# Layer 0 of a four-layer graph network: visiting order of the row tiles, ring of adjacency buffers, first load in pieces

## The chip, the cores and the metric

The kernel runs on one core of one Trainium2 chip. The metric is device time in microseconds (us), the median of several executions of the whole program, which is one launch. The program computes four layers of a graph network; the change touches the first of them.

## The reference, cut to what matters

There are N = 2708 nodes with D = 128 features (x), and a dense 2708 x 2708 float32 matrix adj of which under one per cent is non-zero. Layer 0 is

```python
h = jnp.maximum(_layernorm(x, axis=-1), 0.0)
x = x + _L0_gnn_ref(h, adj)

def _L0_gnn_ref(X, H):
    msg = jnp.matmul(H.T, X)
    inv_deg = 1.0 / H.sum(axis=0)
    inv_deg = jnp.where(jnp.isinf(inv_deg), 0.0, inv_deg)
    return msg * inv_deg[:, None]
```

Layer 1 sums gelu messages over the edges (weights from adj), layer 2 is a GRU cell on adj @ h, and layer 3 is an attention masked by adj > 0. All four read adj: layers 2 and 3 need it transposed, and layer 1 works from lists of its non-zero entries. Layer 0 prepares both forms while it computes its own result.

## The kernel before, in words

adj is cut into 22 row tiles of 128 rows (`NT`); the last, tile 21, has 20 rows. They are visited in `GROUPS`: five sets of four tiles and a last short set of two (20 and 21). For each row tile n layer 0 does five things:

- `load_row_tile(n)` (L254, issued by SyncE, SP) loads 128 x 2708 floats, 1354 KB.
- `aggregate_rows(n, ci)` (L297, TensorE) accumulates msg for six column chunks of at most 512, with the normalised rows `h` as the stationary operand. The six accumulators stay in PSUM for the whole layer.
- `list_row_tile(n)`: for each of 22 column blocks of 124 columns VectorE finds the eight largest values (MAX8, L283) and their positions (FIND_INDEX8, L285). The blocks near the diagonal are read from a copy, `near`, that GpSimd (POOL) makes without the diagonal (L265, L266); POOL also puts the diagonal itself in `dg` (L270). Both tiles have two buffers. The two last row tiles have only their near blocks scanned here; the rest is scanned in layer 1.
- `sign_sums(n)` (L290, L292, ScalarE): counts of non-zero entries, and the diagonal summed from `dg`.
- `turn_blocks(gi, j)`, for each of 22 column tiles j of a set: TensorE transposes one 128 x 128 block of each row tile of the set into a PSUM tile `p_T` (L309; there are two such banks), ScalarE copies it to `aT` and sums it for the degrees (L313), and SP stores it to `adjT` in DRAM (L314). `aT` has eight buffers.

The order on every engine is written out by hand, in `tc.manual_schedule()`. One set after the other is visited. In the first visit all accumulations stand ahead of the transposes; in the others they are interleaved with the 22 steps j. In a visit of four tiles each of steps 1, 6, 11 and 16 issues the scan of one tile, steps 3, 8, 13 and 18 its sign sum, and from the second visit on steps 3, 7, 11 and 15 the load of a tile of the next set. At step 20 `normal_rows` makes the next set's `h` (L137, `hs` in the profile). The first two tiles' scans and sign sums and the sums over x (`sum_rows`, `sum_squares`) stand in the first visit ahead of its transposes.

The row tiles lie in two buffers of a set each (4 x 2708 floats per partition), so the first load of a set waits until all four tiles of the set two visits before are done with. Eight row tiles are loaded at the start, with the rest of x after the second.

The layer ends with the counts of the first four tiles (L350, L352), six copies of the accumulators to `hT`, three by VectorE and three by ScalarE (L355), and the degrees from the sums (L360 to L364), which need the last `aT`. Layer 1 then begins with transposes of `hT` (L767).

The statistics of x for the first four tiles (L118 to L131, with a power on POOL, L121) are issued before, outside the hand-written order; where they stand among the first scans is decided by the scheduler.

Of the kernel before, what the change touches and what calls it, by code (L numbers as in the profile page):

```python
# [20 lines left out]
F32 = mybir.dt.float32  # L21
BF16 = mybir.dt.bfloat16
AF = mybir.ActivationFunctionType
# [7 lines left out]
P = 128  # L31
N = 2708
D = 128
NT = (N + P - 1) // P
# [9 lines left out]
JB = 124  # L44
# [3 lines left out]
GROUPS = [(t, min(4, NT - t)) for t in range(0, NT, 4)]  # L48
# [3 lines left out]
def size(t):  # L52
    return min(P, N - t * P)


def width(b):
    return min(JB, N - b * JB)
# [3 lines left out]
def listed_layers(ctx: ExitStack, tc: tile.TileContext, x, adj, w, out, flag):  # L61
    nc = tc.nc
# [23 lines left out]
    ident = const.tile([P, P], F32, name="ident")  # L86
# [60 lines left out]
    def span(t, k):  # L147

        return t * P, min(k * P, N - t * P)
# [17 lines left out]
    total = keep.tile([P, NT], F32, name="total")  # L167
# [24 lines left out]
    for q in range(2):  # L192
        nc.gpsimd.tensor_copy(xb[q][:, :, 4 * S : 4 * S + R], part.unsqueeze(1).to_broadcast([P, NB, R]))

    LATER = NT - 2
    AT_ONCE = 3
    late_blocks = []
# [7 lines left out]
    with tc.tile_pool(name="l0c", bufs=1) as fix:  # L205
# [29 lines left out]
        def normal_rows(g):  # L235
            t, k = GROUPS[g]
            scale_rows(tiles_of(h, t, k), tiles_of(xs, t, k), rstd[:, t - 4 :], shifts[:, t - 4 :], AF.Relu)

        with (
            tc.tile_pool(name="l0", bufs=2) as rows,  # L240
            tc.tile_pool(name="l0k", bufs=2) as pool,
            tc.tile_pool(name="l0t", bufs=8) as turned,
            tc.tile_pool(name="l0p", bufs=1, space=PSUM) as acc,
        ):
            accs = [acc.tile([P, CH], F32, name=f"acc{c}") for c in range(len(CHUNKS))]
            sets, marks = {}, {}

            def load_row_tile(n):
                gi, q, m = n // 4, n % 4, size(n)
                if q == 0:  # L250
                    sets[gi] = rows.tile([P, 4, N], F32, name="a")
                if m < P:
                    nc.gpsimd.memset(sets[gi][:, q, :], 0.0)
                nc.sync.dma_start(sets[gi][0:m, q, :], adj[n * P : n * P + m, :])  # L254

            def list_row_tile(n):

                m = size(n)
                a = sets[n // 4][:, n % 4, :]
# [10 lines left out]
                nc.gpsimd.tensor_tensor(marks[n][:, 0:m], a[:, d0 : d0 + m], ident[:, 0:m], ALU.mult)  # L270

                def block(b):
                    if b0 <= b <= b1:
                        return near[:, b * JB - c0 : b * JB - c0 + width(b)]
                    return a[:, b * JB : b * JB + width(b)]

                blocks = [b for b in range(NB) if not b0 <= b <= b1] + list(range(b0, b1 + 1))
                if n >= LATER:
                    late_blocks.extend((n, b) for b in range(NB) if not b0 <= b <= b1)
                    blocks = range(b0, b1 + 1)  # L280
                for k in range(0, NB, 2):
                    for b in blocks[k : k + 2]:
                        nc.vector.max(val[:, n, b, :], block(b))  # L283
                    for b in blocks[k : k + 2]:
                        nc.vector.max_index(col[:, n, b, :], val[:, n, b, :], block(b))  # L285

            def sign_sums(n):
                m = size(n)
                sign = pool.tile([P, N], BF16, name="sign")
                nc.scalar.activation(sign, sets[n // 4][:, n % 4, :], AF.Sign, accum_out=total[:, n : n + 1])  # L290
                dg = marks.pop(n)[:, 0:m]
                nc.scalar.activation(dg, dg, AF.Copy, accum_out=own[:, n : n + 1])  # L292

            def aggregate_rows(n, ci):
                c, cw = CHUNKS[ci]
                m = size(n)
                nc.tensor.matmul(  # L297
                    accs[ci][:, 0:cw], h[0:m, n, :], sets[n // 4][0:m, n % 4, c : c + cw],
                    start=(n == 0), stop=(n == NT - 1),
                )  # L300

            def turn_blocks(gi, j):
                g0, gk = GROUPS[gi]
                i0, iw = span(g0, gk)
                k = size(j)
                p = bank("p_T")
                for q in range(gk):
                    m = size(g0 + q)
                    nc.tensor.transpose(  # L309
                        p[0:k, q * P : q * P + m], sets[gi][0:m, q, j * P : j * P + k], ident[0:m, 0:m]  # L310
                    )
                aT = turned.tile([P, CH], F32, name="aT")
                nc.scalar.activation(aT[0:k, 0:iw], p[0:k, 0:iw], AF.Copy, accum_out=sums[0:k, j, gi : gi + 1])  # L313
                nc.sync.dma_start(adjT[0:k, j, i0 : i0 + iw], aT[0:k, 0:iw])  # L314

            with tc.manual_schedule():
                for n in range(8):
                    load_row_tile(n)
                    if n == 1:
                        load_rest()  # L320
                for gi, (g0, gk) in enumerate(GROUPS):
                    steps = [(n, ci) for n in range(g0, g0 + gk) for ci in range(len(CHUNKS))]
                    ahead = gi == 0
                    for n in range(g0, g0 + gk):
                        if ahead:
                            for ci in range(len(CHUNKS)):
                                aggregate_rows(n, ci)
                        if n < 2:
                            list_row_tile(n)
                            sign_sums(n)  # L330
                            (sum_rows, sum_squares)[n](pool)
                    done = 0
                    for j in range(NT):
                        turn_blocks(gi, j)
                        now = len(steps) * (j + 1) // NT if gk == 4 else min(len(steps), j + 1)
                        for step in steps[done:now]:
                            if not ahead:
# [12 lines left out]
                nc.vector.tensor_scalar(some4, val[:, 0:4, :, :], 0.0, None, ALU.is_gt)  # L350
                with nc.allow_low_precision("counts up to 8"):
                    nc.vector.reduce_sum(rows_n[:, 0:4, :], some4, AX.X)  # L352
                for ci, (c, cw) in enumerate(CHUNKS):
                    copy = nc.vector.tensor_copy if ci % 2 == 0 else nc.scalar.copy
                    copy(sumT[:, c : c + cw], accs[ci][:, 0:cw])  # L355
# [543 lines left out]
    accs = ctx.enter_context(tc.tile_pool(name="l23p", bufs=1, space=PSUM))  # L899
# [814 lines left out]
```

## Time and profile before

| | us |
|---|---|
| median of 3 runs | 1063.11 (1061.25 to 1065.79) |
| the profiled execution | 1066.37 |
| its span, first to last instruction | 1064.6 |
| layer 0, to the last degree (L364) | 216.7 |
| end of the scans (L285) | 205.57 |
| end of the transposes (L309) | 214.9 |
| end of the last copy aT (L313) | 215.45 |

Mean granted TensorE clock over the span: 0.946. Over the whole span TensorE's matmuls are busy for 930 us, VectorE for 826, ScalarE for 516, GpSimd for 402.

In a line of the timeline the columns are the start, the duration, engine, line, operation, output and input with shapes, and how many instructions were merged; in brackets stands the idle time before it and what ended it. PE is TensorE, PEld its weight loads, DVE VectorE, ACT ScalarE, POOL GpSimd; SPq is SyncE's queue of DMA issues. In a line of the waits stand the waiting instruction, what it waited for, the total in us, how many times, and the longest. "issue" is time in which an engine waited for nothing that the profile shows.

### The profile page before, as it was taken

How to read it: one execution, taken by the hardware profiler on the slowest of the kernel's cores; microseconds unless marked ns; L12 is line 12 of the kernel's file. 1: busy time of each engine (PE TensorE's matmuls, PEld its weight loads, DVE VectorE, ACT ScalarE, POOL GpSimd, SP SyncE). 2: the span in 40 equal slices, each digit the busy share in tenths (PEclk: the TensorE clock that was granted, in tenths of full speed). 3: DMA queues.
4: the chain of work that ended last, by engine and by line, in shares of the span. 5: the costliest groups of instructions: out<-in, count | busy, mean ns of one | idle time of the engine just before them, and what ended most of it. 6: DMA issues, size and time to landing. Idle time of an engine off the chain costs nothing. (4 is left out here: it accounts for less than half of the span.)

```text
span 1064.6 us, 22002 instructions
## 1 busy us (share of the span) xinstructions
PE 929.8 (87%) x7950; PEld 749.6 (70%) x7950; DVE 826.0 (78%) x2853; ACT 515.7 (48%) x1428; POOL 402.1 (38%) x486
## 2 busy tenths in 40 slices
PE   5788889943799999999999959999989999999983
PEld 2454455432699999899999924444478899989982
DVE  7999999868577798887878264655678987997793
ACT  7787787534766666666666521433322200230142
POOL 3310112022776657666766163344311200250042
PEclk9999999756899999999999979999989999999996
DMA  9888997221233423222231066556410000000000
GB/s 366 305 316 288 320 354 256 77 62 55 77 106 122 125 91 111 100 93 88 91 103 57 28 211 207 196 184 226 124 38 21 8 8 1 2 16 6 1 11 19
DMA packets 60626, 129.67 MB, mean 122 GB/s; under 512 B 11161, under 2 KB 23829, under 8 KB 57799
## 3 DMA queue, kind: packets, MB, share of 16 engines
q1 hardware_dynamic: 58690, 125.38, 34.5%
q10 hardware_dynamic: 1816, 2.80, 1.0%
q8 instruction: 64, 1.05, 0.4%
q14 instruction: 56, 0.45, 0.1%
HBM read 81.55 MB, written 30.87 MB: 106 GB/s over the span
## 5 line engine op out<-in xcount | busy, mean ns | idle before, releaser
L960 PE MATMUL att<-hv,wt 128*128 128x129 f32 x1672 | 194.4, 277 | 8.7 <-DVE wt L930 8.7
L960 PEld LDWEIGHTS att<-hv,wt 128*128 128x128 f32 x1672 | 190.9, 193 | 11.7 <-DVE wt L930 8.6
L539 POOL TENSOR_SCALAR put<-mine,value 128x128 f32<-128x128 bf16 x176 | 149.6, 866 | 69.1 <-DVE mine L436 51.4
L615 PE MATMUL p_m<-s,sel 128*128 128x128 bf16 x1452 | 160.8, 219 | 5.4 <-ACT g L627 5.4
L619 PE MATMUL p_m<-d,cols 124*128 124x128 bf16 (+1 forms) x1452 | 161.2, 219 | 1.3 <-DVE cols L569 1.2
L930 DVE SCALAR_TENSOR_TENSOR wt<-row,lift,mask 128x1024 f32<-128x1024 f32 (+1 forms) x132 | 138.7, 1081 | 23.3 <-PE att L960 23.3
L121 POOL TENSOR_TENSOR n_r<-n_r,minus_half 128x4 f32<-128x4 f32 (+1 forms) x31 | 46.3, 1492 | 270.8 <-DVE n_r L120 265.2
L640 PE MATMUL agg<-put,g 128*128 128x128 f32 (+1 forms) x968 | 135.9, 281 | 0.0
L297 PE MATMUL acc<-a,hs 128*128 128x512 f32 (+2 forms) x264 | 124.5, 574 | 11.2 <-ACT hs L137 11.2
L1099 PE MATMUL p_agg<-a,hs 128*128 128x512 f32 (+2 forms) x264 | 110.5, 561 | 13.0 <-DMA a<-adjT 12.9
L309 PEld LDWEIGHTS p_T<-ident,a 128*128 128x128 f32 x484 | 59.6, 143 | 88.3 <-issue 40.1
L640 PEld LDWEIGHTS agg<-put,g 128*128 128x128 f32 x968 | 118.2, 192 | 0.0
L615 PEld LDWEIGHTS <-sel 128*128 128x128 bf16 x1452 | 104.7, 98 | 9.7 <-issue 7.1
L285 DVE FIND_INDEX8 col<-val,a 128x8 uint16<-128x124 f32 (+1 forms) x400 | 104.8, 269 | 0.0
L309 PE MATMUL p_T<-ident,a 128*128 128x128 f32 x484 | 81.8, 287 | 26.2 <-ACT aT L313 20.0
L619 PEld LDWEIGHTS <-cols 124*128 124x128 bf16 (+1 forms) x1452 | 102.0, 97 | 1.9 <-DVE cols L569 1.9
L627 ACT ACTIVATE g<-p_m 128x512 f32<-128x512 f32 x132 | 73.0, 553 | 61.6 <-PE p_m L619 61.6
L547 ACT ACTIVATE put<-mine,value 128x128 f32<-128x128 bf16 x308 | 100.5, 391 | 0.0
L313 ACT ACTIVATE aT<-p_T 128x512 f32<-128x512 f32 (+2 forms) x132 | 71.1, 541 | 46.9 <-ACT aT L313 31.4
L283 DVE MAX8 val<-a 128x8 f32<-128x124 f32 (+1 forms) x400 | 90.1, 261 | 1.9 <-DMA a<-in_adj 1.9
L1099 PEld LDWEIGHTS p_agg<-a,hs 128*128 128x128 f32 (+1 forms) x264 | 47.8, 195 | 61.9 <-issue 53.0
L297 PEld LDWEIGHTS acc<-a,hs 128*128 128x128 f32 (+1 forms) x264 | 44.7, 202 | 26.7 <-issue 15.3
(260 smaller groups left out, 1504.4 us busy)
## 6 DMA issues: line engine op xcount, KB each, us to landing
a<-in_adj SPq DMA_DIRECT2D x21, 1354.0 KB
adjT<-aT SPq DMA_DIRECT2D x105, 256.0 KB
a<-adjT SPq DMA_DIRECT2D x20, 1280.0 KB
spread<-passed SPq DMA_DIRECT2D x22, 704.0 KB
later<-sel SPq DMA_DIRECT2D x22, 616.0 KB
row<-own_d ACTq DMA_DIRECT2D x10, 256.0 KB
later<-sel SPq DMA_DIRECT2D x22, 82.5 KB
adjT<-aT SPq DMA_DIRECT2D x21, 74.0 KB
```

What stands on the lines that cost most here:

```text
L283: nc.vector.max(val[:, n, b, :], block(b))
L285: nc.vector.max_index(col[:, n, b, :], val[:, n, b, :], block(b))
L297: nc.tensor.matmul(accs[ci][:, 0:cw], h[0:m, n, :], sets[n // 4][0:m, n % 4, c : c + cw], start=(n == 0), stop=(n == NT - 1),)
L309: nc.tensor.transpose(p[0:k, q * P : q * P + m], sets[gi][0:m, q, j * P : j * P + k], ident[0:m, 0:m])
L539: nc.gpsimd.tensor_scalar(st["put", 0][:, b, :], st["mine"][:, b, :], st["value"][:, b : b + 1], None, ALU.mult)
L547: nc.scalar.activation(st["put", 1][:, b - HP, :], st["mine"][:, b, :], AF.Identity, scale=st["value"][:, b : b + 1])
L615: nc.tensor.matmul(p[:, b - b0, :], st["sel"][:, b, :], s3[:, q, t % 2, :], start=(q == 0), stop=False)
L619: nc.tensor.matmul(p[:, b - b0, :], st["cols"][0:kb, b, :], d3[0:kb, b, q, :], start=False, stop=(q == 2))
L640: nc.tensor.matmul(agg, g[:, b - 4 * k, :], put, start=(b == 0), stop=False)
L930: nc.vector.scalar_tensor_tensor(wt[:, 0:n], row[:, k, c : c + n], lift[:, j, k : k + 1], mask[:, j, c : c + n], op0=ALU.max, op1=ALU.mult,)
L960: nc.tensor.matmul(banks[s // 3][:, s % 3, :], wt[:, q * P : (q + 1) * P], hv[:, j, k, :], start=(v < 2 and s // 3 not in touched), stop=( ...
L1099: nc.tensor.matmul(pa[:, 0:n], h[0:k, j, :], a[0:k, j - j0, 0:n], start=(j == 0), stop=(j == NT - 1))
```

## The change

Three things, all in layer 0:

- The short set (tiles 20 and 21) is visited second, and then the other four sets of four tiles in their order. The accumulation's start and stop flags follow the new order.
- The two buffers of a set each become a ring of eight buffers of one row tile. The first eight tiles in the new order (0 to 3, 20, 21, 4, 5) are loaded at the start. After that a load is issued at steps 3, 7, 11 and 15 of a visit only as far as tiles of visits already finished have left a buffer: 6 to 9 in the second visit, 10 and 11 in the third, 12 to 15 in the fourth, 16 to 19 in the fifth.
- Row tile 0 is loaded in four pieces, three of 744 columns and one of 476.

With tile 21 in the first eight, the memset of its buffer stands at the start of POOL's work. Lines behind the change are numbered up to ten higher.

```diff
+    RING = 8
...
-            tc.tile_pool(name="l0", bufs=2) as rows,
+            tc.tile_pool(name="l0", bufs=RING) as rows,
...
             def load_row_tile(n):
-                gi, q, m = n // 4, n % 4, size(n)
-                if q == 0:
-                    sets[gi] = rows.tile([P, 4, N], F32, name="a")
+                m = size(n)
+                tiles[n] = rows.tile([P, N], F32, name="a")
                 if m < P:
-                    nc.gpsimd.memset(sets[gi][:, q, :], 0.0)
-                nc.sync.dma_start(sets[gi][0:m, q, :], adj[n * P : n * P + m, :])
+                    nc.gpsimd.memset(tiles[n], 0.0)
+                step = 6 * JB if n == 0 else N
+                for c in range(0, N, step):
+                    k = min(step, N - c)
+                    nc.sync.dma_start(tiles[n][0:m, c : c + k], adj[n * P : n * P + m, c : c + k])
...
-                    start=(n == 0), stop=(n == NT - 1),
+                    start=(n == order[0]), stop=(n == order[-1]),
...
+            visits = [GROUPS[0], GROUPS[-1]] + GROUPS[1:-1]
+            order = [n for t, k in visits for n in range(t, t + k)]
...
-                for n in range(8):
+                for i, n in enumerate(order[:RING]):
                     load_row_tile(n)
-                    if n == 1:
+                    if i == 1:
                         load_rest()
-                for gi, (g0, gk) in enumerate(GROUPS):
+                freed, loaded = 0, RING
+                for v, (g0, gk) in enumerate(visits):
+                    gi = g0 // 4
...
-                    ahead = gi == 0
+                    ahead = v == 0
...
-                        if gi > 0 and j % 4 == 3 and j < 16 and g0 + 4 + j // 4 < NT:
-                            load_row_tile(g0 + 4 + j // 4)
-                        if j == NT - 2 and gi + 1 < len(GROUPS):
-                            normal_rows(gi + 1)
+                        if j % 4 == 3 and j < 16 and loaded < min(NT, RING + freed):
+                            load_row_tile(order[loaded])
+                            loaded += 1
+                        if j == NT - 2 and v + 1 < len(visits):
+                            normal_rows(visits[v + 1][0] // 4)
+                    freed += gk
```

More of the change, by code (lines that the diff above doesn't have):

```diff
@@ L245, in listed_layers @@
             accs = [acc.tile([P, CH], F32, name=f"acc{c}") for c in range(len(CHUNKS))]
-            sets, marks = {}, {}
+            tiles, marks = {}, {}
             def load_row_tile(n):
-                gi, q, m = n // 4, n % 4, size(n)
-                if q == 0:
-                    sets[gi] = rows.tile([P, 4, N], F32, name="a")
+                m = size(n)
+                tiles[n] = rows.tile([P, N], F32, name="a")
                 if m < P:
-                    nc.gpsimd.memset(sets[gi][:, q, :], 0.0)
-                nc.sync.dma_start(sets[gi][0:m, q, :], adj[n * P : n * P + m, :])
+                    nc.gpsimd.memset(tiles[n], 0.0)
[3 more added lines that the diff above has]
+                    nc.sync.dma_start(tiles[n][0:m, c : c + k], adj[n * P : n * P + m, c : c + k])
             def list_row_tile(n):
                 m = size(n)
-                a = sets[n // 4][:, n % 4, :]
+                a = tiles[n]
                 d0 = n * P
@@ L289, in sign_sums @@
                 sign = pool.tile([P, N], BF16, name="sign")
-                nc.scalar.activation(sign, sets[n // 4][:, n % 4, :], AF.Sign, accum_out=total[:, n : n + 1])
+                nc.scalar.activation(sign, tiles[n], AF.Sign, accum_out=total[:, n : n + 1])
                 dg = marks.pop(n)[:, 0:m]
@@ L297, in aggregate_rows @@
                 nc.tensor.matmul(
-                    accs[ci][:, 0:cw], h[0:m, n, :], sets[n // 4][0:m, n % 4, c : c + cw],
-                    start=(n == 0), stop=(n == NT - 1),
+                    accs[ci][:, 0:cw], h[0:m, n, :], tiles[n][0:m, c : c + cw],
+                    start=(n == order[0]), stop=(n == order[-1]),
                 )
@@ L309, in turn_blocks @@
                     nc.tensor.transpose(
-                        p[0:k, q * P : q * P + m], sets[gi][0:m, q, j * P : j * P + k], ident[0:m, 0:m]
+                        p[0:k, q * P : q * P + m], tiles[g0 + q][0:m, j * P : j * P + k], ident[0:m, 0:m]
                     )
```

## The prediction, on record before the changed kernel was run

> **What bounds the kernel now.** The change touches layer 0 alone (0 to about 217 us), and the page's chain of waits follows only the last microsecond, so layer 0 has to be read from its own windows. First the table by stage: from 201.5 us, where the last pair of row tiles is in work, VectorE has work for only half the stretch and TensorE runs at half clock.
>
> ```profile
> 155.00:189.00 34.00, 29.29 (x141) 17.48 (x140) 34.00 (x231) 26.97 (x67) 7.33 (x13) 1.00 0.74 256
> 189.00:201.50 12.50, 12.08 (x40) 5.26 (x39) 12.50 (x86) 7.09 (x26) 1.24 (x3) 1.00 0.30 94
> 201.50:215.00 13.50, 13.40 (x34) 5.77 (x32) 7.14 (x33) 7.16 (x29) 0.68 (x3) 0.50 0.22 64
> ```
>
> (Columns after the length: PE, PEld, DVE, ACT, POOL, granted clock, DMA share, GB/s.) Second, VectorE's timeline at the end: the scans end at 205.57, then it waits 6.78 us for ScalarE's last copy aT before it can form the degrees.
>
> ```profile
> 205.31 0.26 DVE L285 FIND_INDEX8 col<-val,near 128x8 uint16<-128x104 f32 x1
> ...
> 206.84 1.88 DVE L355 COPY hT<-acc 128x512 f32<-128x512 f32 x3
> 215.49 0.29 DVE L360 TENSOR_REDUCE deg<-sums 128x22 f32<-128x132 f32 x1 [6.78 <-ACT aT L313]
> ```
>
> Third, TensorE's timeline there: no gaps, but a 20-row accumulation pair takes 2.05 us where four us earlier it took 1.10.
>
> ```profile
> 198.24 1.10 PE L297 MATMUL acc<-a,hs 20*128 20x512 f32 x2
> ...
> 202.95 2.05 PE L297 MATMUL acc<-a,hs 20*128 20x512 f32 x2
> ...
> 208.74 6.16 PE L309 MATMUL p_T<-ident,a 128*128 128x128 f32 x20
> ```
>
> Fourth, the waits of 0 to 217 us (total, times, longest):
>
> ```profile
> PEld p_T L309 <- ACT aT L313: 38.8, 50, 2.9
> ...
> PEld p_T L309 <- DMA a<-in_adj: 6.9, 3, 2.6
> DVE deg L360 <- ACT aT L313: 6.8, 1, 6.8
> ...
> DVE val L283 <- DMA a<-in_adj: 1.9, 1, 1.9
> ...
> ACT dg L292 <- POOL dg L270: 1.0, 1, 1.0
> ```
>
> So the end of layer 0 is set by the pair TensorE/ScalarE (transpose, copy, two PSUM buffers), which waits for the scans 1.0 us in all. VectorE is full from 7.4 to 205.6 but ends ten us early. Reordering removes no work from the pair; that is the heart of the forecast.
>
> **What the Trainium skill says.** "TensorE: Matmul & The Clock Gate", Part 1: the array falls to half clock after an idle window of about 3.4 us and returns after a busy one. The trace agrees roughly at 89 us: after a 2.3 us wait for a row tile, one step is cold.
>
> ```profile
> 89.74 0.60 ACT L313 ACTIVATE aT<-p_T 128x512 f32<-128x512 f32 x1 [2.31 <-issue]
> 92.30 0.60 ACT L313 ACTIVATE aT<-p_T 128x512 f32<-128x512 f32 x1 [1.87 <-issue]
> 93.72 0.60 ACT L313 ACTIVATE aT<-p_T 128x512 f32<-128x512 f32 x1 [0.73 <-ACT aT L313]
> ```
>
> A step is 1.30 us; here the two take 2.56 and 1.42, so one cold start costs 1.4. But at 201.7 the clock falls while TensorE is busy; what changed there is the height, 20 rows of 128. Part 4 of that page says transposes don't count as busy in the same way; the trace agrees only in part, since transposes alone ran at clock 1.00 from 33 to 47 us. "ScalarE: Activation LUTs", "What ACT_TABLE_LOAD costs": 1283 ns; the trace shows 1.28. "DMA: Bandwidth & Descriptors", "Anatomy of one DMA": some 2 us of a transfer are fixed, mostly completion; the trace has x's first piece issued at 0.72 and used at 4.05.
>
> **The change part by part.**
>
> *Four pieces.* The DMA table at 1.5 us slices gives 407 to 419 GB/s from 3 us on; xs (0.26 MB) fills up to 3.0 and is used at 4.05, so a byte is usable 1.05 us after it has moved. The first piece (128 x 744 floats, 0.38 MB) is then usable at about 4.9, the last at 7.4, as the whole tile is now. VectorE is busy with the statistics of x to 5.28, so it scans from 5.3, not 7.36. But in the changed program's order ten blocks (4.5 us) stand ahead of the statistics' last steps, so n_r comes at about 11.7 (now 10.6). On ScalarE the table load (1.28) stands behind three of the piece waits, where now it is done at 2.0: the first sign sum runs 8.7 to 11.3. The first hs so starts at 11.8 instead of 10.63: **+1.2 us** for TensorE's start (bounds 0 to 2.5). SP issues three more DMAs (0.48 each); tile 1 comes 1.4 us later, with 9 us of slack.
>
> *The memset of tile 21* (2.36 us on POOL, now at 166.5) moves ahead of the first near: tile 0's dg comes 2.5 us later, ScalarE waits for it, and behind it stand the sums of x and the rsqrt on POOL. ScalarE's 5.10 us of idling before 33.09 cover it. Tile 2's near comes at 36.2 where VectorE wants it at 35.2: one us, on VectorE only.
>
> *The order.* A visit, from its first hs to the next one's, took 31.6 us (from 53.63), 35.8, 34.2, 33.6; the short one 26.7 to its last copy, 26.1 to where the next hs would be. The three long ones each waited for a fourth row tile (2.3, 2.2, 1.6). After: tiles 6 and 7 are loaded at steps 3 and 7 of the short visit, 8 to 11 even earlier against theirs, so only the visits of 12 to 15 and 16 to 19 keep that wait. From 54.8 (53.63 + 1.2): short visit to 80.9, tiles 4-7 with one cold step 33.0 to 113.9, 8-11 31.6 to 145.5, then twice 33.9 (mean of 34.2 and 33.6) to 213.3, and the last copy ends 0.6 later, **213.9, now 215.45: -1.55**. This keeps the half clock inside the short visit, because the same 20-row products stand there.
>
> *The scans.* near(n) queues on POOL behind dg(n-1), which waits for ScalarE's dg(n-3). VectorE does a tile in 9.75 us (POOL's near at 184.75, 194.50, 204.25). It begins tile 4 at 48.6 and tile 7 at 77.9; it wants near(7) at 86.8. near(7) waits for ScalarE's dg of tile 4: visit start 80.9 + 9.0 (62.65 less 53.63) + 1.4 = 91.3, so 92.7 with POOL's 1.4. VectorE stalls 5.9 us, which its own ten us of slack pay: twelve more tiles end at 210.6, and with 1.4 us of counting it is at 212.0, still before 213.9. It gets no second stall (near(8) at 100.1, wanted 102.5).
>
> *The ring.* The same 8 x 10,832 bytes per partition. Loads into it wait tile by tile; those of tiles 6 to 9 wait for the scans of 0 to 3 (done by 46.9) and are issued at some 62 to 78, so SP's stores behind them are not held. The later layers' weight loads move ahead of stores on SP (0.4 to 0.5 us each), under the same cover. Cost nothing; cover: at least 15 us; if it were gone, the copies would stop eight steps later, when the aT buffers run out.
>
> *The exit.* The last accumulations now come after the last transposes: +0.4 before hT is copied. TensorE arrives there at full clock: eight transposes take 1.1 instead of 1.97; msg_wT's load behind 256 KB stores takes some of that back: -0.7 (bounds -1.5 to +1).
>
> Sum: -1.55 + 0.4 - 0.7 = **-1.9 us**. Against the profiled execution's own 1066.37 (span 1064.6 and 1.8 around it) that is 1064.5; that execution is 3.3 us above the median of 1063.11, within the runs' spread, so the median becomes 1061.2. About 0.5% (5.3 us) is what a measurement of this kernel can tell from no change.
>
> **Rivals.**
>
> *A, the short visit stays at full clock.* Busy neighbours on both sides might hold the clock. Its cold part (202.4 on: 12.5 us) would take two steps of 1.37, 0.65, and ten copies at 0.45, 7.9: -4.6, and the cold start behind it goes, -1.4. Then near(7) is in time, scans end at 204.6, and ScalarE ends at 207.9: 1055.2. Against it: the clock fell at 201.7 with full visits just before. 0.20.
>
> *B, slower: cold TensorE is carried into the visit of tiles 4-7.* Each cold step there costs 1.26 us. From -1.9 it takes six further cold steps (7.6) to be slower by over 5.3: 1069. For it: once down, the clock stayed at 0.50 from 201.7 to 233. Against it: at 89 us one dense window brought it back. 0.18.
>
> *C, the split or the ring does nothing, or VectorE's new stall is longer than its slack.* VectorE and ScalarE both hang on the start of the visit of 4-7, so their ends move together: within 2 us of the forecast; I leave it in the main case.
>
> **How the numbers follow.** Main case 0.62, its own range 1058 to 1065; A 0.20 (faster), B 0.18 (slower). The range 1055 to 1069 leaves out about half of A and half of B.
>
> **What would show it.** Right: the last aT near 214; clock 0.5 inside the second visit (about 68 to 82 us) and one or two cold steps after; a VectorE wait on near of some 6 us near 87 us; two waits for a fourth row tile; first hs near 11.8. Wrong: VectorE's degrees waiting for scans rather than for aT, no half clock in the second visit (A), or half clock past 90 us (B).

## The result, and the profile after

The change makes the kernel slower by 0.37%: the ratio to the kernel before, measured beside it, is 1.0037, 95% interval [1.0026, 1.0048]. That is 3.9 us more (the two medians, 1067.57 and 1064.2 us, lie 3.4 us apart). It is inside the 0.5% named in the prediction, but clear of zero and on the other side of the forecast of -1.9 us. The profiled execution took 1072.5 us (span 1070.7) and is one of four of its 20 executions between 1071 and 1074; the others lie between 1065.8 and 1068.8. So a time read from its trace lies about 5 us above the median, and the ledger below sets other profiles with the same order beside it.

The table by stage of the changed kernel (columns as before: PE, PEld, DVE, ACT, POOL, clock, DMA share, GB/s). The short visit, 57.5 to 88, and the start of the next one:

```profile
57.50:69.00 11.50, 11.08 (x32) 4.53 (x31) 11.50 (x79) 6.52 (x24) 1.38 (x4) 0.85 0.50 152
69.00:88.00 19.00, 17.01 (x39) 7.06 (x39) 18.58 (x125) 7.84 (x32) 1.24 (x3) 0.50 0.78 249
88.00:94.00 6.00, 5.77 (x18) 3.53 (x19) 2.10 (x15) 3.44 (x13) 0.00 (x0) 0.60 0.81 286
```

The half clock that stood at the end of the layer now stands inside the second visit, as forecast. New is the DMA share: 0.50 and then 0.78, where the old short visit had 0.30 and then 0.22, because row tiles are loaded beside it. TensorE's timeline shows the products of 20 rows doubling in time, and then, before the first transposes of the next visit, a wait for ScalarE:

```profile
67.62 1.10 PE L300 MATMUL acc<-a,hs 20*128 20x512 f32 x2
68.65 0.55 PE L312 MATMUL p_T<-ident,a 128*128 128x128 f32 x2
69.04 2.05 PE L300 MATMUL acc<-a,hs 20*128 20x512 f32 x2
...
88.23 1.12 PE L312 MATMUL p_T<-ident,a 128*128 128x128 f32 x4 [2.21 <-ACT aT L316]
```

The waits of 0 to 224 us (total, times, longest) name what ScalarE waited for: stores of aT, a wait that was not in the list before.

```profile
DVE val L286 <- POOL near L269: 11.4, 2, 9.8
...
ACT aT L316 <- DMA adjT<-aT: 4.4, 2, 2.4
PE p_T L312 <- DMA a<-in_adj: 4.1, 2, 2.2
```

VectorE's wait for near is there (9.8 us), and the waits for a fourth row tile are two instead of three. VectorE's timeline at the end shows that the degrees still wait for ScalarE's last aT, only 8 us later than before:

```profile
217.72 0.29 DVE L288 FIND_INDEX8 col<-val,near 128x8 uint16<-128x124 f32 x1
...
223.47 0.29 DVE L370 TENSOR_REDUCE deg<-sums 128x22 f32<-128x132 f32 x1 [2.65 <-ACT aT L316]
```

The start, last. Three things are needed to read it: `n_r` holds the factors of the layer norm with which ScalarE makes hs, `offdiag` is one minus the identity, from which GpSimd makes near, and ACT_TABLE_LOAD is what ScalarE does once ahead of its first activation. In the kernel before, the first hs came at 10.63:

```profile
7.13 2.44 POOL L190 MEMSET later<- 128x2816 bf16 x1
...
8.33 1.33 DVE L207 TENSOR_SCALAR offdiag<-ident 128x128 f32<-128x128 f32 x1
...
10.63 1.65 ACT L137 ACTIVATE hs<-xs,n_r 128x128 f32<-128x128 f32 x4 [0.72 <-DVE n_r L131]
```

In the changed kernel it comes at 14.52:

```profile
8.90 1.28 ACT L293 ACT_TABLE_LOAD   x1 [8.90 <-DMA a<-in_adj]
...
10.11 3.15 DVE L208 TENSOR_SCALAR offdiag<-ident 128x128 f32<-128x128 f32 x1
10.20 2.46 ACT L293 ACTIVATE sign<-a 128x2708 bf16<-128x2708 f32 x1
...
10.36 2.89 DVE L128 TENSOR_TENSOR n_r<-n_r 128x4 f32<-128x4 f32 x1
...
10.82 2.35 POOL L253 MEMSET a<- 128x2708 f32 x1
...
14.52 1.65 ACT L137 ACTIVATE hs<-xs,n_r 128x128 f32<-128x128 f32 x4 [1.77 <-DVE n_r L131]
```

The last piece of tile 0 lets ScalarE go at 8.90, the table load stands behind it, the sign sum ends at 12.66, and hs then waits 1.77 us more for n_r. VectorE's offdiag, one pass over 128 x 128, took 3.15 us and ended at 13.26, when GpSimd's memset of tile 21 had ended at 13.17; the last steps of n_r stand behind it. The profile before had this in small already: offdiag took 1.33 us there and ended at 9.66, just behind GpSimd's memset of `later`, which ended at 9.57.

### The profile page after: what moved, and what is told of

The parts are those of the page before. It is cut to its first block, busy times and chain, and to the rows that moved or that the text cites. A ratio compares the mean times of both kernels' runs of the same rounds, so it can differ in the third digit from the quotient of the medians.

```text
span 1070.7 us, 22025 instructions
## 1 busy us (share of the span) xinstructions
PE 933.5 (87%) x7950; PEld 751.6 (70%) x7950; DVE 829.0 (77%) x2853; ACT 515.3 (48%) x1428; POOL 401.2 (37%) x486
## 5 line engine op out<-in xcount | busy, mean ns | idle before, releaser
L970 PEld LDWEIGHTS att<-hv,wt 128*128 128x128 f32 x1672 | 191.8, 194 | 11.8 <-DVE wt L940 8.6
L300 PE MATMUL acc<-a,hs 128*128 128x512 f32 (+3 forms) x264 | 128.9, 592 | 15.1 <-DMA xs<-in_x 15.1
L312 PEld LDWEIGHTS p_T<-ident,a 128*128 128x128 f32 (+1 forms) x484 | 60.7, 145 | 90.8 <-issue 44.3
L1109 PE MATMUL p_agg<-a,hs 128*128 128x512 f32 (+2 forms) x264 | 109.9, 558 | 12.1 <-DVE n1u_r L120 6.1
L288 DVE FIND_INDEX8 col<-val,a 128x8 uint16<-128x124 f32 (+1 forms) x400 | 107.7, 283 | 0.0
L312 PE MATMUL p_T<-ident,a 128*128 128x128 f32 (+1 forms) x484 | 83.1, 291 | 25.7 <-ACT aT L316 21.7
L286 DVE MAX8 val<-a 128x8 f32<-128x124 f32 (+1 forms) x400 | 94.8, 280 | 0.9 <-DMA a<-in_adj 0.9
L300 PEld LDWEIGHTS acc<-a,hs 128*128 128x128 f32 (+1 forms) x264 | 45.8, 207 | 30.6 <-ACT hs L137 15.1
```

Of the source, the lines that this page charges most:

```text
L300: nc.tensor.matmul(accs[ci][:, 0:cw], h[0:m, n, :], tiles[n][0:m, c : c + cw], start=(n == order[0]), stop=(n == order[-1]),)
L312: nc.tensor.transpose(p[0:k, q * P : q * P + m], tiles[g0 + q][0:m, j * P : j * P + k], ident[0:m, 0:m])
L970: nc.tensor.matmul(banks[s // 3][:, s % 3, :], wt[:, q * P : (q + 1) * P], hv[:, j, k, :], start=(v < 2 and s // 3 not in touched), stop=( ...
L1109: nc.tensor.matmul(pa[:, 0:n], h[0:k, j, :], a[0:k, j - j0, 0:n], start=(j == 0), stop=(j == NT - 1))
```

## The experiments

Three theories are tested. Theory 1 (T1): TensorE and ScalarE bound the layer, and they lose by a later start and by a longer short visit. Theory 2 (T2): VectorE's new wait for near bounds it. Theory 3 (T3): it is chance in when the clock falls and rises. All ratios are to the kernel before, measured on the same chip. The profiles give these times (us):

| kernel | first hs | 2nd visit begins | short visit | degrees begin | ratio [95%] |
|---|---|---|---|---|---|
| before | 10.63 | 53.63 | 26.7 | 215.49 | 1 |
| pieces_only | 12.70 | 54.63 | 26.5 | 217.62 | 1.0029 [1.0018, 1.0039] |
| before_tall | 10.26 | 52.30 | 24.8 | 211.97 | 0.9975 [0.9965, 0.9986] |
| before_start | 7.61 | 53.16 | 26.1 | 212.57 | 1.0006 [0.9993, 1.0020] |
| before_best | 7.58 | 53.25 | 20.1 | 210.68 | 0.9956 [0.9941, 0.9971] |
| before_best_aT12 | 7.64 | 50.24 | 24.6 | 210.63 | 0.9952 [0.9935, 0.9969] |
| after | 14.52 | 57.51 | 30.6 | 223.47 | 1.0037 [1.0026, 1.0048] |
| order_ring_only | 10.29 | 52.98 | 29.0 | 216.16 | 1.0012 [0.9998, 1.0025] |
| after_memset_late | 12.83 | 54.93 | 31.5 | 219.87 | 1.0030 [1.0019, 1.0041] |
| after_offdiag_pool | 12.47 | 54.48 | 28.7 | 216.65 | 1.0038 [1.0022, 1.0053] |
| after_near_deep | 14.07 | 56.78 | 28.0 | 219.55 | 1.0046 [1.0029, 1.0062] |
| after_stats_first | 9.79 | 53.04 | 28.5 | 217.65 | 1.0029 [1.0009, 1.0048] |
| after_tall | 12.92 | 55.69 | 26.5 | 218.34 | 1.0020 [1.0009, 1.0031] |
| after_aT12 | 12.10 | 53.89 | 28.3 | 215.71 | 1.0011 [0.9998, 1.0024] |
| after_tall_aT12 | 12.16 | 54.99 | 21.7 | 210.87 | 0.9956 [0.9938, 0.9974] |
| order_tall_aT12 | 10.27 | 52.12 | 20.8 | 207.67 | 0.9914 [0.9895, 0.9932] |
| after_best | 7.59 | 50.72 | 20.7 | 206.69 | 0.9920 [0.9900, 0.9941] |
| after_best_whole | 7.66 | 50.51 | 21.4 | 207.56 | 0.9915 [0.9898, 0.9932] |

(In the old order the short visit is the last; there its length is read from its hs to the degrees.) One profile is one execution, a ratio is from 6 to 22 executions: the times say where, the ratios how much. The difference of two ratios is uncertain by 1.6 to 2.8 us, most where there are fewest executions.

### The parts of the change

**pieces_only.** The kernel before with

```diff
-                nc.sync.dma_start(sets[gi][0:m, q, :], adj[n * P : n * P + m, :])
+                step = 6 * JB if n == 0 else N
+                for c in range(0, N, step):
+                    k = min(step, N - c)
+                    nc.sync.dma_start(sets[gi][0:m, q, c : c + k], adj[n * P : n * P + m, c : c + k])
```

> The kernel before with only the four pieces of tile 0 added. Theories: T1, the pair TensorE/ScalarE bounds layer 0, so the loss is its later start (first hs 14.5 us instead of 10.6) plus a longer short visit (30.6 us instead of the 26.1 reckoned). T2, the new 9.8 us wait of VectorE for near in the visit of tiles 4-7 bounds it. T3, nothing but chance in when the clock warms up. Here ten scan blocks still stand ahead of the statistics' end and the ACT table load stands behind the piece waits, but there is no early memset of tile 21. T1: first hs at 11.5 to 12.5 us, last aT 1 to 2 us later than before's 215.5, total 1.000 to 1.002 of before. T2 and T3: no change of the end (1.000), VectorE gains up to 2 us that nobody waits for.

Measured: 1.0029, or 3.1 us, more than expected; the profiled start moved by 2.07 us and the degrees by 2.13. Its timeline at the start:

```profile
8.95 1.28 ACT L293 ACT_TABLE_LOAD   x1 [8.95 <-DMA a<-in_adj]
...
10.07 0.22 DVE L207 TENSOR_SCALAR offdiag<-ident 128x128 f32<-128x128 f32 x1
...
12.70 1.63 ACT L137 ACTIVATE hs<-xs,n_r 128x128 f32<-128x128 f32 x4
```

Without the early memset offdiag takes 0.22 us and n_r is ready at 11.83. It is ScalarE that is late: it waits for the last piece, then does the table load, then the sign sum, one behind the other. VectorE's scans ended two us earlier (203.8) and nothing waited for them. Theories 2 and 3 had expected no change.

**order_ring_only.** The changed kernel with tile 0 loaded whole:

```diff
-                step = 6 * JB if n == 0 else N
+                step = N
```

> The changed kernel with tile 0 loaded whole: order and ring alone. T1: the scan blocks and the table load stand again as before, so the first hs is back at 10.6 to 12 us (the memset of tile 21 still runs on POOL near the statistics and may hold their last step), while the short visit in second place stays near 30 us; the total is 1 to 3 us under the changed kernel's, about 1.001 of before. T2: the near wait of VectorE stays near 10 us, so the total stays at the changed kernel's (1.0035 of before). T3: anywhere within 1.000 to 1.004.

Measured: 1.0012, 2.7 us less than the change as a whole. So the pieces cost about 3 us in either order. Order and ring together cost about 1 us, which is not clear of zero (interval -0.2 to 2.7), where -3.1 was forecast for them. The wait for near was still 7.2 us here.

### The start

**after_memset_late.** The loads of tiles 21, 4 and 5, and with them the memset, are issued after the scan of tile 0:

```diff
-                for i, n in enumerate(order[:RING]):
+                for i, n in enumerate(order[:5]):
...
                             list_row_tile(n)
+                            if n == 0:
+                                for late_n in order[5:RING]:
+                                    load_row_tile(late_n)
```

> The changed kernel with the loads of tiles 21, 4 and 5, and so the memset of tile 21, issued behind the scan of tile 0: the memset leaves the statistics' stretch. T1: offdiag takes about 1.3 us or less again instead of 3.15, n_r comes at about 11.7 and the first hs at about 12 instead of 14.5; everything behind it moves up by the same, total 2 to 3 us under the changed kernel's, 1.001 of before. T2: the wait for near later on is unchanged, so the total is the changed kernel's, 1.0035 of before. T3: 1.0035, with no shift that follows the first hs.

Measured: first hs 12.83, but a ratio of 1.0030 where theory 1 expected 1.001: the 0.7 us against the change lie inside the intervals.

**after_offdiag_pool.**

```diff
-        nc.vector.tensor_scalar(offdiag, ident, -1.0, 1.0, ALU.mult, ALU.add)
+        nc.gpsimd.tensor_scalar(offdiag, ident, -1.0, 1.0, ALU.mult, ALU.add)
```

> The changed kernel with offdiag formed by GpSimd instead of VectorE; tile 21's memset stays at the start of GpSimd's work. It tests why n_r came at 14.5 us. In four profiles offdiag ended within 0.1 us of the end of a long GpSimd memset (9.66 after 9.57, 9.31 after 9.24, 9.29 after 9.20, 13.26 after 13.17). T1a, only offdiag is held by the memset, and n_r stands in order behind it: n_r comes at about 11.8, the first hs follows the sign sum at 12.7 to 12.9, the layer's end and the total fall by 1.7 us against the changed kernel, ratio to before about 1.002. T1b, every VectorE instruction is held while that memset runs: n_r at 13.5 or later, the first hs near 14.5, the ratio stays 1.0035. T2 (the near wait bounds): ratio 1.0035.

Measured: first hs at 12.47 and n_r at 11.45, as T1a says, and a ratio of 1.0038, as it does not. The other profiles show why this one could not tell: the same start is in after_near_deep, after_tall, after_aT12 and after_tall_aT12, and in the last three offdiag took 0.21 to 0.22 us with nothing done about it. With the change's own these are five profiles, and a hold of over 2 us came in two of them, the change's and after_near_deep's; in the second it fell on another TENSOR_SCALAR, the one inside the statistics:

```profile
9.78 0.22 DVE L208 TENSOR_SCALAR offdiag<-ident 128x128 f32<-128x128 f32 x1
...
10.26 2.90 DVE L129 TENSOR_SCALAR n_r<-n_r 128x4 f32<-128x4 f32 x1
...
10.78 2.36 POOL L254 MEMSET a<- 128x2708 f32 x1
```

Here L129 began together with the first of GpSimd's four memsets (10.26) and ended with the last. In after_aT12 it began at 9.91, ahead of them, and took 0.21 us; in after_tall it began at 10.74, inside such a run, and came through in 0.26. So the hold differs from one execution to the next. If it comes in two of five executions, 2 us each, it is 0.8 us on average, less than these ratios can show.

**after_stats_first.** offdiag on GpSimd as above, and the statistics put first by hand:

```diff
-    normalise(h, xs, 0, 4, AF.Relu, "n0")
+    n0 = moments(tiles_of(xs, 0, 4), "n0")
...
             with tc.manual_schedule():
+                scale_rows(tiles_of(h, 0, 4), tiles_of(xs, 0, 4), *factors(*n0), AF.Relu)
```

> The changed kernel with the start put in another order: the statistics of x ahead of the scan blocks on VectorE, the first hs ahead of tile 0's sign sum on ScalarE, offdiag on GpSimd. The four pieces and the memset stay. T1, the pair's start sets the end: n_r at about 8, the first hs at 8.0 to 8.5 and TensorE's first product at 8.5 to 9.0 when tile 0's last piece lands; every later visit 6 us earlier than in the changed kernel, total 5 to 6.5 us lower, ratio to before 0.997 to 0.999. T2 and T3: an earlier start is lost at the near wait or in the clock's chance, ratio 1.002 to 1.004.

Measured: first hs 9.79, not 8.0: L129 met the other long memset (6.76, 2.46 us). The second visit began at 53.04, 4.5 us earlier than in the profile of the change, yet the ratio is 1.0029 in only eight executions. Theory 1's expectation for the total, 0.997 to 0.999, failed; the interval reaches down to 1.0009, so how much of the start came through is not told.

**before_start.** The kernel before with the pieces, after_stats_first's edits, and GpSimd's memset of `later` moved behind the small ones:

```diff
-    nc.gpsimd.memset(later, 0.0)
...
         nc.gpsimd.memset(sums, 1.0)
+        nc.gpsimd.memset(later, 0.0)
```

> The kernel before with the four pieces and another order at the start: statistics of x ahead of the scan blocks on VectorE, the first hs ahead of tile 0's sign sum on ScalarE, offdiag on GpSimd, and GpSimd's long memset (later) moved behind the small ones, so that no VectorE TENSOR_SCALAR of the statistics runs beside it. It tests the start alone, in the old order of visits. T1, the start of the pair sets the end: n_r at 7.5, first hs at 7.6 and first product at 8.1 to 8.9 (before: 10.63 and 11.18), total 2 to 3 us under before, 0.997 to 0.998. If the first visit's transposes are bound by ScalarE's sums over x instead (these end at 28 us and need 18 us after the first sign sum): the first aT copy moves up by less than 1 us, total 0.999 to 1.001. If the pieces cost something besides the start: at or above 1.001.

Measured: first hs at 7.61, TensorE's first product at 8.16, and 1.0006. A start 3 us earlier gains nothing measurable here. Most of it was gone by the second visit already: the first visit took 45.5 us instead of 43.0, with 2.8 us of ScalarE waiting for a store of aT (at 37.55) while row tiles were still being loaded (DMA share 1.06 from 36 to 38 us). So in these runs a first hs later than that of the kernel before costs, and an earlier one does not gain.

### VectorE's wait

**after_near_deep.** `near` and `dg` from a pool of their own with five buffers (both tiles are then taken from `nearpool`):

```diff
             tc.tile_pool(name="l0t", bufs=8) as turned,
+            tc.tile_pool(name="l0n", bufs=5) as nearpool,
```

> The changed kernel with five buffers each for near and dg instead of two, so that GpSimd can make the near copies ahead. It asks whether VectorE's wait of 9.8 us at 90 us costs time. T2: yes; the wait goes, and the total falls by 2 to 4 us against the changed kernel, ratio to before 1.000 to 1.001. T1: no; the wait goes or shrinks below 2 us and the scans end up to 9 us earlier (near 209), but VectorE then waits that much longer for the last aT, which stays within 1 us of 223.3 less what the clock's chance gives; ratio 1.003 to 1.004.

Measured: the scans end at 208.6 instead of 218.0, the waits list holds no wait of VectorE for near of over 0.2 us, and the ratio is 1.0046. Theory 2 falls. What VectorE gained it waits off at the end, for the accumulators (5.6 us) and for aT (2.6).

### The short visit

**before_tall.** Tile 21's rows above 20 are zero, so its products and transposes can run over 128 rows:

```diff
             def aggregate_rows(n, ci):
...
-                m = size(n)
+                m = P
...
             def turn_blocks(gi, j):
...
-                    m = size(g0 + q)
+                    m = P
```

> The kernel before, with tile 21's products and transposes over 128 rows (108 of them zero) instead of 20. It asks what drops TensorE's clock in the short visit. If it is the 20-row operands: clock 1.00 from 189 us to the end of the layer, pairs of products stay at 1.10 us, the short visit's last copy is about 4.6 us earlier (near 211), VectorE's 6.8 us wait for it shrinks to some 2, total 0.996 of before. If it is the short visit itself (fewer columns per step): clock 0.50 from 201.7 as before, total 1.000 to 1.001.

Measured: 0.9975, or 2.7 us. The last stage of the table of this kernel, which stood at clock 0.50 before, and TensorE's timeline for the fourth and fifth pair of tile 21, which took 2.05 us each in the kernel before:

```profile
201.50:211.50 10.00, 5.62 (x25) 3.06 (x24) 6.75 (x31) 4.61 (x28) 0.68 (x3) 0.83 0.26 76
```

```profile
199.70 1.02 PE L297 MATMUL acc<-a,hs 128*128 128x512 f32 x2
200.56 0.38 PE L309 MATMUL p_T<-ident,a 128*128 128x128 f32 x2
200.78 1.02 PE L297 MATMUL acc<-a,hs 128*128 128x512 f32 x2
```

The pairs stay at 1.02 us, so the clock no longer falls while TensorE is at work: the height of the operands is what dropped it. It still fell once, from 206 to 209 us, but after TensorE had waited 3.5 us for ScalarE. The cleanest sight of it is in order_tall_aT12 below, where the clock is 1.00 from 56 us to the end of the short visit. The height costs something at full clock too: from 190 to 201 us a step of one pair and its two transposes took 1.33 to 1.38 us before and takes 1.08 now. So the 2.7 us are not the clock's alone, and how they divide was not tested. In the profile the last copy came 3.5 us earlier.

**after_tall.** The same edit on the changed kernel.

> The changed kernel with tile 21's products and transposes over 128 rows instead of 20. In the kernel before the same edit gave 0.9975. T1: the clock stays at 1.00 through the short visit in second place but for a cold start, the short visit takes 26 to 27 us instead of 30.6, the following visit starts warm, and the total falls by 3 to 5 us against the changed kernel, ratio to before 0.999 to 1.000. If the fall of the clock there comes from the visit's waits instead: 0.50 from 69 us as now, ratio 1.0035.

Measured: 1.0020, 1.8 us less, under the 3 to 5 expected. ScalarE's timeline says why: at full clock the copies come about 0.48 us apart and run into the stores, twice.

```profile
73.43 0.29 ACT L316 ACTIVATE aT<-p_T 128x148 f32<-128x148 f32 x1
76.34 0.29 ACT L316 ACTIVATE aT<-p_T 128x148 f32<-128x148 f32 x1 [2.52 <-DMA adjT<-aT]
...
81.85 0.29 ACT L316 ACTIVATE aT<-p_T 128x148 f32<-128x148 f32 x1 [3.68 <-DMA adjT<-aT]
```

**after_aT12.**

```diff
-            tc.tile_pool(name="l0t", bufs=8) as turned,
+            tc.tile_pool(name="l0t", bufs=12) as turned,
```

> The changed kernel with twelve aT buffers instead of eight. In every kernel so far that visits the short set second, ScalarE's last copy of that visit waits 2.4 to 3.4 us for the store of the aT tile eight steps earlier (8 buffers). If that wait is what lengthens the short visit: it goes, the short visit falls from 28 to 30.6 us to 26 to 28, the next visit starts warmer, total 2 to 3 us under the changed kernel's, ratio to before about 1.001. If the wait only hides another (the next hs or the transposes behind it): short visit unchanged within 0.5 us, ratio 1.0035.

Measured: 1.0011, 2.8 us less; no wait of ScalarE for a store is left in the list. The visit is still long (28.3, against 28.0 to 31.5 with eight buffers), because it began with three cold steps, steps at half clock (pairs of 2.08 us at 54.87, 57.31 and 59.75) and because half clock paces its last copies, 0.63 us apart:

```profile
76.87 0.29 ACT L316 ACTIVATE aT<-p_T 128x148 f32<-128x148 f32 x1 [0.92 <-ACT aT L316]
77.50 0.29 ACT L316 ACTIVATE aT<-p_T 128x148 f32<-128x148 f32 x1 [0.24 <-ACT aT L316]
```

**after_tall_aT12.** Both edits, the start as changed.

> The changed kernel with only the two cures of the short visit: tile 21 over 128 rows and twelve aT buffers; the start is left as changed (first hs 12 to 14.5). One by one they gave 1.0020 and 1.0011 against 1.0037. If the short visit is the larger part of the loss and its two causes hide each other: short visit 20 to 24 us, as in the version with all cures (20.7), total 6 to 8 us under the changed kernel, ratio 0.996 to 0.998. If they only add: 24 to 26 us, ratio 0.9995.

Measured: 0.9956, 8.6 us under the change, with a short visit of 21.7 us. One by one the cures gave 1.8 and 2.8, 4.6 together: each limit stood behind the other.

**order_tall_aT12.** The same with tile 0 loaded whole.

> The same two cures with tile 0 loaded whole. It asks what the four pieces cost once the short visit is cured. If the later start is carried through to the end: 2 to 3 us under the one with pieces, ratio 0.994 to 0.996. If the pieces cost nothing there: equal to it.

Measured: 0.9914, 4.5 us less again, more than the 2 to 3 expected for a later start. With after_best and after_best_whole, from which it can't be told apart, this is the fastest version, about 9 us under the kernel before. Its TensorE at the end of the short visit does twenty transposes in 4.67 us, where the change needed 6.16:

```profile
65.77 1.02 PE L300 MATMUL acc<-a,hs 128*128 128x512 f32 x2
67.21 0.44 PE L312 MATMUL p_T<-ident,a 128*128 128x128 f32 x2 [0.42 <-ACT aT L316]
67.48 0.42 PE L300 MATMUL acc<-a,hs 128*128 128x148 f32 x2
67.74 4.67 PE L312 MATMUL p_T<-ident,a 128*128 128x128 f32 x20
```

### All cures, in both orders

**before_best** is before_start with tile 21 over 128 rows; **before_best_aT12** has twelve aT buffers as well; **after_best** is the changed kernel with before_start's start, 128 rows and twelve buffers; **after_best_whole** is that with tile 0 loaded whole.

> The same as before_start, and tile 21's products and transposes over 128 rows. The edit of the height alone gave 0.9975 (2.7 us). If the two add up: 5 to 6 us under before, 0.995. If the start is not worth anything: 0.9975.

> The old order of visits with all four cures: before_best with twelve aT buffers as well. It asks whether the new order itself is worth anything when both orders have the same cures. If the order is neutral: 0.992 as with the new order. If the order's own terms count (two waits for row tiles instead of three, the exit at full clock) and aT's buffers only mattered for the short visit in the middle: 0.995 to 0.996, as before_best.

> The changed kernel with all four cures: tile 21 over 128 rows, the early start of before_start, the long memset late, twelve aT buffers. T1 (start plus short visit make the loss, the order itself is neutral): first hs near 7.6, short visit 25 to 26.5 us, total 5 to 8 us under the changed kernel, 0.995 to 0.998 of before, within 2 us of before_best. If the order itself costs something else: 1.000 or more. If it saves its two shorter waits for row tiles: 2 us under before_best.

> The version with all four cures (0.992 of before) with tile 0 loaded whole instead of in four pieces. TensorE's first product there began at 8.1 with the last piece landing near 8.9; a whole tile was usable at 7.4. If the pieces bring nothing: first hs 7.6 again, products of tile 0 without a wait, ratio 0.991 to 0.993. If they let VectorE begin early enough to matter at the end of the scans (204 us there): ratio 0.993 to 0.995.

Measured: 0.9956 and 0.9952 in the old order, 0.9920 and 0.9915 in the new one; after_best is below every branch of its expectation, with a short visit of 20.7 us instead of 25 to 26.5. With the same cures the new order is 0.0032 better than the old one (0.9920 against 0.9952), 3.4 us with an uncertainty of 2.8. Once the start does not depend on them, the four pieces neither cost nor gain (0.9920 and 0.9915). The early start brought nothing in the new order either: order_tall_aT12, at 10.27, is as fast. There VectorE has become the end of the layer: its scans end at 204 to 205, and no wait for aT stands before the degrees in after_best and order_tall_aT12.

Twelve buffers bring nothing measurable in the old order, although the second visit of before_best_aT12 begins 3 us earlier than that of before_best. Its waits (total, times, longest) show where those 3 us go:

```profile
POOL near L268 <- DVE col L288: 130.8, 18, 8.4
...
ACT dg L295 <- POOL dg L273: 5.3, 4, 3.0
```

In the old order tile 21 is scanned last. GpSimd can't make its near and dg before VectorE gives back one of the two near buffers, and ScalarE sums that dg ahead of the last 13 copies of aT. In before_best_aT12 ScalarE waits 2.96 us for it, goes on at 203.54, and the copies end 7 us later; in before_tall it waits as long, in before_start 1.86 us, in the kernel before 0.99. So VectorE, which seems to end early, holds the last copies as soon as TensorE and ScalarE are quicker, and what an earlier start or twelve buffers gain is waited off there. In the new order only three copies stand behind the dg of the last tile. This is read from the traces; no run with more near buffers in the old order tested it.

## Why the prediction was wrong, point by point

The ledger of the prediction beside the trace of the change, and beside the other profiles of the new order without a cure of the short visit:

| step | predicted | change's profile | other profiles |
|---|---|---|---|
| first hs | 11.8 | 14.52 | 12.5 to 14.1 with the pieces (9.8 with the statistics first) |
| short visit | 26.1 | 30.56 | 28.0 to 31.5 |
| tiles 4-7 | 33.0 | 33.02 | 32.1 to 33.6 |
| tiles 8-11 | 31.6 | 31.73 | 31.73 to 31.74 |
| tiles 12-15 | 33.9 | 33.83 | 33.6 to 35.6 |
| tiles 16-19, to last aT | 34.5 | 36.8 | 33.9 to 35.1 without a cold step, 37.0 and 37.3 with |
| degrees to first hs of layer 1, against before | about -0.7 | 11.44 against 12.14 | 11.3 to 11.4 |

In the change's profile the three terms that failed make 2.7 + 4.5 + 2.3 = 9.5 us, the whole of 223.4 against 213.9 for the last aT; in the median of the executions they are smaller.

- *The start, +1.2 (bounds 0 to 2.5): mis-sized.* That the last piece is usable "at 7.4, as the whole tile is now" failed: it came at 8.3 to 9.2 (why so late was not tested). Table load and sign sum stand behind it, as foreseen, so the first hs is at 12.1 to 12.9 without a long hold. The order on VectorE was foreseen too, and n_r, due at 11.7, came at 10.7 to 12.1. Not foreseen was that the memset, which the prediction moved and priced only for its followers on GpSimd, can hold an instruction of VectorE: then the first hs is at 14.1 to 14.5. The sign of it was in the profile before, in the 1.33 us of offdiag. The ratios put the pieces at 2.7 to 4.5 us.
- *The short visit, 26.1: mis-sized, and the step that failed is the ring's.* The prediction had said "SP's stores behind them are not held" and "Cost nothing; cover: at least 15 us". The loads were indeed issued in time, but in the visit the stores of aT land late beside them, and the last copy before the next hs waits 2.4 to 3.4 us. In the change's profile the store that it waits for was issued at 81.05, 0.8 us behind a load of 1354 KB, and the copy went on at 87.79. The duration was borrowed from a visit at the end of the layer that began warm and had no loads beside it; the new one also begins with one to three cold steps (a pair at 60.02 takes 2.08 us in the change's profile). That the late stores come from sharing the DMA engines with the row tiles is argued from the DMA share of 0.78; that the eight buffers turn them into a wait is shown by after_aT12.
- *The half clock inside it:* right, in place and in cause; before_tall and order_tall_aT12 show the height of the operands. Whether the products or the transposes do it was not separated. Once both were 128 rows high, the visit was limited by the stores; the prediction, and rival A with it, had only the clock in mind. That rival A's 1055.2 is about what order_tall_aT12 reached (1055.33) is a coincidence: it took both cures.
- *The last visit, +2.3:* after the 2.20 us wait for a row tile at 190.49 one step was cold in this profile; in order_ring_only and after_offdiag_pool the same wait (2.22 and 2.02) cost none. The Trainium skill, "TensorE: Matmul & The Clock Gate", Part 1 ("What's actually happening"), says that the clock follows an activity window of about 3.4 us that runs freely. That the same wait may therefore fall on it in one execution and not in another is our inference; the three traces fit it, with waits that are shorter than the window. The prediction put one such step into the visit of tiles 4-7 and none here.
- *VectorE's wait, 5.9 us, covered:* it was 9.8 us, since near(7) came at 99.9 instead of 92.7 with everything ahead of it late; that it was covered is right, as after_near_deep shows.
- *Two waits for a fourth row tile, the long visits, the exit at full clock:* right.
- *"Reordering removes no work from the pair":* right as it stands. The order's own gain of 3.1 us (-1.55 - 1.2 + 0.4 - 0.7) did not come: order_ring_only is 1.3 us slower than the kernel before, not clear of zero, because the short visit took it away. The two orders with the same cures do differ by 3.4 us (uncertainty 2.8), but that the numbers meet is luck: there the old order ends with ScalarE's copies behind the dg of tile 21 and the new one with VectorE's scans, and neither stands in the prediction's sum.
- *Rival B* (cold TensorE into the visit of tiles 4-7): two cold steps in the change's profile (pairs of 1.91 and 1.57 us at 89.14 and 91.70), and the visit took the 33.0 us that the main case gave it. It was not the cause, though the sign was its own.

What stays open: the four executions above 1071 us (a held start and a cold step in one execution would fit; this is only argued); why the last piece lands later than the whole tile did; and whether an earlier start is worth something in the old order once tile 21 is 128 rows high, since before_best is 2.0 us under before_tall with an uncertainty of 1.9.

## What to carry to other kernels

A duration is borrowed with its surroundings: a visit moved from the end to the middle gets row-tile loads beside it, a cold start ahead of it and stores that must come back before its few buffers turn round; ask for each of these what it costs. A load split so that one engine can begin earlier puts that engine's new work ahead of what another engine waits for, and makes the third wait for the last piece: look for the first hs, not for the first scan. Two limits in one stage hide each other, so test cures in pairs before calling one of them small. And an engine that ends early can still set the end for another, through a buffer that it gives back late: follow the buffers as well as the last instruction.

## What the runs showed of the hardware

VectorE's TENSOR_SCALAR can be held by memsets of GpSimd until they end, even on 128 x 4 elements: it took 0.21 us alone and 2.46, 2.90 and 3.15 us beside them, each time ending within 0.1 us of the memset's end, while MAX8 and FIND_INDEX8 beside the other long memset (6.92 to 9.36 in the change's profile) ran on at 0.28 us or less each. The Trainium skill, "SBUF — State Buffer", "Who interferes with whom", names it: copies, casts and TENSOR_SCALAR can enter a mode that takes the port pair which VectorE shares with GpSimd, and the loser is blocked for the whole instruction. The traces agree. They add that a run of memsets one behind the other can hold it to the end of the run (10.26 to 13.14 in after_near_deep), but need not: in after_tall an L129 that began inside such a run took 0.26 us.

TensorE's clock fell to 0.50 under continuous work when some of its operands were 20 rows high (69 to 88 us of the change's profile), and did not when the same work was done over 128 rows with zeros (1.00 from 56 to 73 us in order_tall_aT12). With the shorter steps at full clock this was worth 2.7 us of 1063 in the old order, for two lines of code.
